# Moving the preparation of the second half of the tokens, one early product and the loads of the last product's h

## The chip, the cores and the metric

The kernel runs on one core of a Trainium2 chip. Its time is the device time of one execution in microseconds; several executions are made, and their median is given. A core has five engines that each work through their own list of instructions in order and wait for each other through semaphores: TensorE (PE in the profile), VectorE (DVE), ScalarE (ACT), GpSimd (POOL) and SyncE (SP), which issues nearly all of this kernel's transfers.

## The reference

For 2048 tokens (2 x 1024) of width 512, in float32:

```python
xn = layernorm(x)                              # no weights
s  = xn @ (weight * block_mask).T              # 512 x 512, mask in blocks of 32 x 32
nx = xn * rsqrt(mean(xn * xn) + 1e-5) * ln_w
h  = silu(nx @ gate_w.T) * (nx @ up_w.T)       # gate_w, up_w: 1792 x 512
g  = silu(h @ down_w.T)                        # down_w: 512 x 1792
out = x + s * g
```

The mask of a block is 1 where any of its elements is above zero. Of `setup_inputs`, what matters is the sizes above.

## The kernel before

**Products.** All matrix products are made with a scheme of seven products in place of eight (a Strassen form), applied twice: an outer level with products q = 1 to 7 and an inner level with products m = 1 to 7. A group g holds 128 rows of gate and 128 of up; there are G = 7 groups, and an eighth (g = G) that is the masked weight. For each group and each q, `instance(j, g, q, ...)` makes seven 128x128 by 128x512 products into PSUM banks called x, y and z (tags X, Y, Z; V is for everything else). j is the place in the order: first q = 1 and 2 for all eight groups (j = 0 to 15), then for each group q = 6, 5, 7, 3, 4. So "x_1" in the text is the bank x of instance j = 1. Within an instance the products have offsets 0, 2, 3, 4, 6, 8 and 12 (m = 1, 5, 2, 6, 3, 7, 4), so that two instances interlace and PE makes one product per position.

**Sums around a product.** After m = 1, `seed` copies x (into bank z for j > 0, so that z accumulates on it; into a slot named s1 for j = 0). `snap` takes a copy of an unfinished bank, plus the sums of the product before (`prior`); `total` adds such copies to the finished bank. With no prior these are ACT copies, else DVE sums. A product that goes on in a bank has to wait for the snapshot out of it.

**Tokens.** The 2048 tokens are four blocks t of 512, each four tiles of 128. A block is prepared by `load_x`, `stats` (DVE), `factors` (which has a square root on ACT), `normalise`, `transpose` (PE, into a bank pt_t_c for each 128 columns c), `evacuate` (ACT), and by sums of blocks, `outer_b` and `inner_b`. Blocks 0 and 1 are needed from the first product on, blocks 2 and 3 from j = 16 on.

**Order.** Nothing is scheduled by a tool. Each step is filed with a position by `at(pos, fn, ...)`, and at the end the steps are issued in the order of their positions; each engine executes its own in that order. One position is about 0.86 us; `T(us)` turns a planned time into a position, and `EARLY` holds positions for single products and seeds of the first instances that differ from the rule. `SILU = 26.2` is the earliest position of a silu.

**The h of the last product.** For each group, h and sums of it are written to `h_dram`. The last product, with `down_w`, loads them by sets (`load_h(q, slots, part)`); its first set, q = 1, comes in six parts: four of 768 KB (b11, b12, b22, b21) and two of 256 KB (e0, e1). SP's list holds these loads among stores of h, loads of each group's weights (`load_block`, L274, from in_gu), of the pieces of down_w (`outer_d`, L499), of the q = 1 and 2 sums (acc_dram, L462) and of h again (L465).

**Slots.** `mem` is one large SBUF tile, cut into slots of 128x512 by name (B1, q, v5 and so on); whoever takes a slot again waits for its readers.

Banks come from a pool with a number for each tag (`PSB`): X has three, Y two, Z one and V two, so a new tile with a tag waits for the readers of an old one.

Of the kernel before, what the change touches and what calls it, by code (L numbers as in the profile page):

```python
# [9 lines left out]
I32 = mybir.dt.int32  # L10
# [21 lines left out]
def tile_masked_linear_gated_ffn(  # L32
# [11 lines left out]
    nc = tc.nc  # L44
# [21 lines left out]
    EARLY = {}  # L66

    def at(pos, fn, *args):
        events.append((pos, len(events), fn, args))
# [5 lines left out]
    mem = big.tile([P, sum(n for _, n in RINGS), W], F32, tag="mem", name="mem")  # L75
# [5 lines left out]
    F = first_slot  # L81
# [11 lines left out]
    def bank(tag, name):  # L93
        return ps.tile([P, W], F32, tag=tag, name=name, bufs=PSB[tag])

    def add(eng, o, a, b, op=ALU.add):
        eng.tensor_tensor(o, a, b, op)  # L97

    dve, pool, act = nc.vector, nc.gpsimd, nc.scalar
# [68 lines left out]
    def rms_factor():  # L168

        def first():  # L170
            nc.vector.tensor_scalar_add(rms, agg[:, :, :, 1], EPS)
            nc.vector.reciprocal(rms, rms)
            nc.vector.tensor_mul(rms, agg[:, :, :, 1], rms)
            nc.vector.tensor_scalar_add(rms, rms, EPS)
        return [first, lambda: nc.scalar.activation(rms, rms, AF.Sqrt)]
# [115 lines left out]
    mrows = {}  # L291

    def load_mask(R, K):
        mrows[R, K] = mem[:, F["v5"] + 2 * R + K, :].bitcast(I32)
        nc.sync.dma_start(mrows[R, K], mask[R, K])

    mask_sums = small.tile([P, 4, 16], F32, tag="mask_sums", name="mask_sums", bufs=1)
# [35 lines left out]
    def instance(j, g, q, prior, dest, after):  # L333


        st = {}

        seeded = j > 0

        def mm(m, tag, key, first):  # L340
            if first and key not in st:
                st[key] = bank(tag, f"{key}_{j}")
            nc.tensor.matmul(st[key], weights(g, q, m), operand(q, m), start=first and not (key == "z" and seeded),  # L343
                             stop=True, skip_group_check=True)

        def seed():

            if seeded:
                st["z"] = bank("Z", f"z_{j}")
                nc.scalar.copy(st["z"], st["x"])  # L350
            else:
                st["s1"] = slot("s2", f"s1_{j}")
                nc.scalar.copy(st["s1"], st["x"])

        def snap(key, name, i):
            s = st[name] = slot(name, f"{name}_{j}")
            if prior is None:
                nc.scalar.copy(s, st[key])
            else:
                add(dve, s, st[key], prior(i))  # L360

        def total(key, name, i):
            if key == "z" and not seeded:
                name = "s1"
            if name:
                add(dve, dest(i), st[key], st[name])
            elif prior is None:
                nc.scalar.copy(dest(i), st[key])
            else:
                add(dve, dest(i), st[key], prior(i))  # L370

        at(EARLY.get((j, 0), 7 * j + 1), seed)
        for off, m, tag, first, snapshot, out in (
            (0, 1, "X", True, None, None),
            (2, 5, "Y", True, ("s5", 3), None),
            (3, 2, "Z", True, None, (None, 0)),
            (4, 6, "X", False, ("s2", 1), None),
            (6, 3, "Y", False, None, ("s2", 1)),
            (8, 7, "X", False, None, ("s5", 3)),
            (12, 4, "X", False, None, (None, 2)),  # L380
        ):
            key, pos = tag.lower(), 7 * j + off
            at(EARLY.get((j, m), pos), mm, m, tag, key, first)
            if snapshot:
                at(pos + 1, snap, key, *snapshot)
            elif out:

                pos += 2.3 if prior is None and m == 2 and seeded else 1
                at(pos, total, key, *out)
                after(out[1], pos)  # L390

# [278 lines left out]
    N = len(order)  # L670
    END = 7 * N
    T = lambda us: (us - 14.9) / 0.86
    EARLY.update({(0, 1): T(11.5), (0, 0): T(12.6), (1, 1): T(12.7), (0, 2): T(12.8)})
    SILU = 26.2
    at(T(-10), load_x, 0)
    at(T(-10), lambda: nc.sync.dma_start(lnw_sb, ln_w))
# [10 lines left out]
    def plan(pos, step, todo):  # L687
        for i, fn in enumerate(todo):
            at(pos + step * i, fn)
# [4 lines left out]
            nc.tensor.matmul(b[:, :P], ident, ident, start=True, stop=True, skip_group_check=True)  # L694

    at(T(1.4), lambda: warm(30, bank("V", "idle")))
    for t, p, step in ((0, T(8.2), 0), (1, T(13.4), 0), (2, 14.5, 1.3), (3, 22.0, 1.3)):
        plan(p, step, factors(t))
    for i in range(TT):
        half = act if i < 2 else dve  # L700
        at(T(4.5 + 0.85 * i), stats, 0, i)
        at(T(9.0 + 0.7 * (i % 2)), normalise, 0, i, half)
        at(T(10.1 + 0.8 * i), stats, 1, i)
        at(T(14.2 + 0.7 * (i % 2)), normalise, 1, i, half)
        for c in range(KC):
            at(T((10.2, 10.6, 11.0, 11.8)[c] + 0.1 * i), transpose, 0, c, (2, 3, 0, 1)[i], "XYYX"[c])
            at(T(15.3 + 0.4 * c + 0.1 * i), transpose, 1, c, (2, 3, 0, 1)[i], "XVVY"[c])
    at(T(6.0), scale_a, 0, 0, pool)
    at(T(8.2), scale_a, 0, 1, pool)
    for c in range(KC):  # L710
        at(T((10.7, 11.3, 11.9, 14.0)[c]), evacuate, 0, c, act)
        at((5.6, T(16.0), 6.0, 3.14)[c], evacuate, 1, c, act)
    for us, q, m in ((15.9, 1, 5), (16.6, 1, 6), (17.2, 1, 7), (17.8, 2, 5), (18.4, 1, 4), (19.0, 2, 6),
                     (19.6, 2, 7), (20.3, 2, 4)):
        at(T(us), inner_b, q, m, dve)
    for q in (1, 2):
        for k in (0, 1):
            for n in (0, 1):
# [1 line left out]
    at(T(16.4), scale_a, 1, 0)  # L720
    at(5.2, scale_a, 1, 1)
    for i in range(TT):
        at(9.6 + 1.2 * i, stats, 2, i)
        at(17.2 + 1.3 * i, stats, 3, i)
        at((30.2, 37.0, 40.9, 44.0)[i], normalise, 2, i, act)
        at(26.5 + 2.4 * i, normalise, 3, i, dve)
    plan(22.2, 1.3, rms_factor())

    for t, p0 in ((3, 37.5), (2, 51.5)):
        n = t % 2  # L730
        for k, c in enumerate((2, 3, 0, 1)):
            for i in range(TT):
                at(p0 + 2 * k + 0.01 * i, transpose, t, c, i, "V")
            if c >= 2:
                at(p0 + 2 * k + 1.2, evacuate, t, c, act)
            else:
                at(p0 + 2 * k + 1.2, outer_b, 5, c, n, dve)
                at(p0 + 2 * k + 1.21, outer_b, 7, c, n, dve)
    for k in (0, 1):
        for n in (0, 1):  # L740
            at(58, outer_b, 3, k, n, None)
    for n, p0 in ((1, 46), (0, 60)):
        for k in (0, 1):
            at(p0 + 1.5 * k, outer_b, 6, k, n, dve)
            at(p0 + 2.2 + 1.7 * k + (16 if n == 1 else 4), outer_b, 4, k, n, pool)
    for q, p in ((6, 63), (5, 70), (7, 78), (4, 90), (3, 113)):
        for off, m, eng in ((0, 5, dve), (3, 6, dve), (5.5, 7, pool), (7.5, 4, pool)):
            at(p + off, inner_b, q, m, eng)

# [29 lines left out]
        for off, fn in zip((8, 24.6, 26.05, 26.06, 26.07, 27.5, 30), outer_d(f)):  # L779
            at(7 * where[f, BLOCKS[0]] + off, fn)  # L780
    for i, (R, K) in enumerate(QUADS):
        at(62, load_mask, R, K)
        at(68 + 1.5 * i, mask_rows, R, K)
    at(79.5, mask_blocks)
    at(120, rms_store)
    for t in range(NTT):
# [17 lines left out]
    QD, later = (F["a1"] + 4, F["acc"], F["s"] + 5), {}  # L804
    for o, q in enumerate(DOWN):
        if o == 0:
            parts = [(p, 7 * where[4, 6] + 4 * k) for k, p in enumerate((b11, b12, b22, b21, e0, e1))]
        elif o == 1:
            parts = [(p, END - 22 + 7 * p[0]) for p in (b11, b21, e0, b12, b22, e1)]
        else:  # L810
            d = D(o - 2)
            parts = [(b11, d(4)), (b12, d(4) + 0.1), (b21, d(14)), (b22, d(21)), (e0, d(25) + 1), (e1, d(25) + 1.1)]
        for part, pos in parts:
            at(pos, load_h, q, (H0, H1)[o % 2], part)
        for k, m in enumerate((5, 6, 7, 4)):
            if o:
                at(D(o - 1)((3, 8, 12, 18)[k]) + 0.3, inner_h, q, m, TS[(4 * o + k + 3) % 5])
            elif m in (6, 4):
                at(END + {6: -1.95, 4: 7.5}[m], inner_h, q, m, first_t[m])
        if o == 0:  # L820
            for k in range(K3):
                in_bank, sums = first_h(q, k, first_t[5], first_t[7])
                at(END - 24.4 + 7 * k, in_bank)
                at(END - 22.95 + 7 * k, sums)
        at((END - 29.8, END - 14, END + 7)[o] if o < 3 else D(o - 2)(4), load_d, q, QD[o % 3])

        def weight_sums(q=q, i=F["q"] + 2 - 3 * (o % 2), o=o):
            for k, fn in enumerate(inner_d(q, i)):
                later[o, k] = fn
        for k in range(4):  # L830
            pos = END + (-6, -4.8, 2, 4)[k] if o == 0 else D(o - 1)(10) + 2.5 * k
            if k == 0:
                at(pos, weight_sums)
            at(pos, lambda o=o, k=k: later[o, k]())
# [81 lines left out]
```

## Time and profile before

| | us |
|---|---|
| median of 3 runs | 516.2 (515.59 to 516.71) |
| the profiled execution, its time | 516.81 |
| the profiled execution, its span | 515.0 |
| PE busy | 507.4 |
| DVE busy | 383.6 |
| POOL busy | 339.3 |
| ACT busy | 179.3 |

The span is from the first to the last instruction; the time has what lies around it too. TensorE's granted clock is at full speed in all of it. In the profile a product of 128x512 is two matmul instructions[...]. "L97" is a line of the kernel before; many sums have that one line, that of the helper `add`. In the time line, a row can hold several instructions of a kind that follow each other (x2 and so on).

### The profile page before, as it was taken

To read this page: it belongs to the slowest core of one execution; us is meant where nothing else is said; L and a number is where in the kernel's file an instruction comes from. 1 tells how busy PE (TensorE), PEld (TensorE's weight loads), DVE (VectorE), ACT (ScalarE), POOL (GpSimd) and SP (SyncE) were. 2 spreads that over 40 slices of the span, in tenths; PEclk is the share of its full clock that TensorE was granted. 3 is DMA by queue.
4 is the path that set the end of the run, shared out by engine and by line. 5 is a ranking of instruction groups with operands and counts; after the bars stand their busy time and mean duration, and the time that the engine had idled before them with its cause. 6 is when DMAs were issued, how large, how long until landed. Compare 5 with 4: busy or idle time off the path is not lost. (4 is left out here: it accounts for less than half of the span.)

```text
span 515.0 us, 4942 instructions
## 1 busy us (share of the span) xinstructions
PE 507.4 (99%) x1277; PEld 231.5 (45%) x1277; DVE 383.6 (74%) x587; ACT 179.3 (35%) x343; POOL 339.3 (66%) x280
## 2 busy tenths in 40 slices
PE   8999999999999999999999999999999999999997
PEld 8444544444444444444434444444444444444444
DVE  5898789766986969789596978978846655467726
ACT  3657554642536344353533524331100101001111
POOL 5422229952695978869598799977653654739960
PEclk9999999999999999999999999999999999999999
DMA  8335456459157584676987568399997699466472
GB/s 311 139 123 204 164 200 232 181 215 325 73 208 223 223 285 178 229 247 198 357 342 272 198 228 282 144 316 397 348 357 275 190 352 342 158 253 204 156 233 82
DMA packets 60460, 121.59 MB, mean 236 GB/s; under 512 B 5760, under 2 KB 13328, under 8 KB 58384
## 3 DMA queue, kind: packets, MB, share of 16 engines
q1 hardware_dynamic: 60144, 120.75, 66.1%
q10 hardware_dynamic: 288, 0.52, 0.3%
q8 instruction: 10, 0.16, 0.2%
q14 instruction: 18, 0.15, 0.1%
HBM read 75.11 MB, written 46.15 MB: 235 GB/s over the span
## 5 line engine op out<-in xcount | busy, mean ns | idle before, releaser
L97 POOL TENSOR_TENSOR mem<-mem 128x512 f32<-128x512 f32 (+4 forms) x243 | 303.6, 1271 | 139.0 <-ACT mem L264 45.6
L343 PE MATMUL x<-mem 128*128 128x512 f32 x448 | 214.3, 595 | 1.1 <-DVE mem L97 1.0
L343 PEld LDWEIGHTS x<-mem 128*128 128x128 f32 x448 | 83.4, 190 | 108.7 <-issue 85.2
L97 DVE TENSOR_TENSOR mem<-x,mem 128x512 f32<-128x512 f32 x136 | 92.1, 685 | 41.1 <-PE x L343 40.0
L343 PE MATMUL y<-mem 128*128 128x512 f32 x224 | 114.5, 592 | 0.1
L97 DVE TENSOR_TENSOR mem<-mem 128x512 f32<-128x512 f32 (+3 forms) x62 | 78.7, 1277 | 6.9 <-PE dx L586 3.6
L586 PE MATMUL dx<-mem 128*128 128x512 f32 x174 | 78.3, 592 | 0.0
L97 DVE TENSOR_TENSOR mem<-y,mem 128x512 f32<-128x512 f32 x96 | 65.8, 685 | 11.0 <-PE y L343 9.5
L343 PEld LDWEIGHTS y<-mem 128*128 128x128 f32 x224 | 42.2, 190 | 52.6 <-issue 47.4
L350 ACT COPY z<-x 128x512 f32<-128x512 f32 x55 | 31.5, 573 | 96.8 <-PE x L343 89.4
L343 PE MATMUL z<-mem 128*128 128x512 f32 x112 | 57.5, 594 | 0.7 <-ACT z L350 0.7
L586 PEld LDWEIGHTS dx<-mem 128*128 128x128 f32 x174 | 33.1, 190 | 41.6 <-issue 40.7
L586 PE MATMUL dy<-mem 128*128 128x512 f32 x98 | 44.5, 592 | 0.0
L404 ACT ACTIVATE gate<-mem 128x512 f32<-128x512 f32 x56 | 33.1, 601 | 28.2 <-DVE mem L97 23.8
L409 DVE TENSOR_TENSOR mem<-gate,mem 128x512 f32<-128x512 f32 x56 | 38.2, 683 | 4.4 <-POOL mem L97 4.2
L559 POOL TENSOR_TENSOR mem<-mem 128x512 f32<-128x512 f32 x16 | 24.7, 1545 | 16.7 <-DMA mem<-s_dram 16.6
L343 PEld LDWEIGHTS z<-mem 128*128 128x128 f32 x112 | 20.9, 190 | 26.8 <-issue 23.4
L569 ACT ACTIVATE silu<-mem 128x512 f32<-128x512 f32 x15 | 9.0, 602 | 64.6 <-DVE mem L97 48.3
L97 DVE TENSOR_TENSOR mem<-z,mem 128x512 f32<-128x512 f32 x41 | 28.0, 684 | 3.6 <-PE z L343 3.6
L586 PEld LDWEIGHTS dy<-mem 128*128 128x128 f32 x98 | 18.6, 190 | 23.4 <-issue 23.2
L97 DVE TENSOR_TENSOR mem<-dx,mem 128x512 f32<-128x512 f32 x16 | 11.1, 691 | 20.1 <-PE dx L586 20.1
L586 PE MATMUL dz<-mem 128*128 128x512 f32 x56 | 25.2, 592 | 0.0
(72 smaller groups left out, 286.7 us busy)
## 6 DMA issues: line engine op xcount, KB each, us to landing
h_dram<-mem SPq DMA_DIRECT2D x98, 256.0 KB, 2.1
mem<-h_dram SPq DMA_DIRECT2D x28, 768.0 KB, 6.7
mem<-in_gu SPq DMA_DIRECT2D x42, 256.0 KB, 4.7
acc_dram<-mem SPq DMA_DIRECT2D x8, 1024.0 KB, 4.3
mem<-acc_dram SPq DMA_DIRECT2D x8, 1024.0 KB, 4.8
s_dram<-mem SPq DMA_DIRECT2D x16, 256.0 KB, 5.0
mem<-s_dram SPq DMA_DIRECT2D x16, 256.0 KB, 6.6
mem<-in_x_t SPq DMA_DIRECT2D x16, 256.0 KB, 6.3
```

Source lines behind the costliest of these rows:

```text
L97: eng.tensor_tensor(o, a, b, op)
L343: nc.tensor.matmul(st[key], weights(g, q, m), operand(q, m), start=first and not (key == "z" and seeded), stop=True, skip_group_check=True)
L350: nc.scalar.copy(st["z"], st["x"])
L404: nc.scalar.activation(gate[key], t(), AF.Silu)
L409: nc.vector.tensor_mul(a(), gate[key], b())
L559: at_later.append(lambda: nc.gpsimd.tensor_tensor(s_tile, s_tile, rms_bc[t], ALU.mult))
L569: nc.scalar.activation(b[0][:, part], y[:, part] if source is None else source(), AF.Silu)
L586: nc.tensor.matmul(st[key], w(), b(), start=first and key != "z", stop=True, skip_group_check=True)
```

## The change

It does these things:

- All of the preparation of blocks 2 and 3 (stats, factors, normalise, transposes, sums) is filed later, most of it by 14 positions. Their square roots thereby come after the first silu. The mask's rows are loaded earlier, into slots of the name q, and reduced with more distance.
- z of instance 1 (`(1, 2)` in `EARLY`) is made in the first gap, after z of instance 0. It starts afresh in a Y bank, and is no longer seeded; x of instance 1 is instead added, with the prior, to a slot by a DVE sum (`seed`), and `total` of z is filed at position 7.0. The copy of pt_0_3 is filed earlier for it. pt_1_3 goes to a V bank, and its transposes come a little later. Two of the sums `inner_b` of q = 1 and 2 go from DVE to POOL.
- The six parts of h of the first set are loaded one per group behind the groups' weights: b11, b12, b22 and b21 with groups 1 to 4, e0 and e1 with group 5.

The diff, cut to its core (in unchanged order):

```diff
-        mrows[R, K] = mem[:, F["v5"] + 2 * R + K, :].bitcast(I32)
+        mrows[R, K] = mem[:, F["q"] + 2 * R + K, :].bitcast(I32)
...
-        seeded = j > 0
+        seeded = j > 1
...
-                st[key] = bank(tag, f"{key}_{j}")
+                st[key] = bank("Y" if key == "z" and j == 1 else tag, f"{key}_{j}")
...
-                nc.scalar.copy(st["s1"], st["x"])
+                if prior is None:
+                    nc.scalar.copy(st["s1"], st["x"])
+                else:
+                    add(dve, st["s1"], st["x"], prior(0))
...
+                if m == 2:
+                    pos = EARLY.get((j, "z"), pos)
...
-    EARLY.update({(0, 1): T(11.5), (0, 0): T(12.6), (1, 1): T(12.7), (0, 2): T(12.8)})
+    EARLY.update({(0, 1): T(11.5), (0, 0): T(12.6), (1, 1): T(12.7), (0, 2): T(12.8), (1, 2): T(12.9),
+                  (1, 0): 4.5, (1, "z"): 7.0})
...
-    for t, p, step in ((0, T(8.2), 0), (1, T(13.4), 0), (2, 14.5, 1.3), (3, 22.0, 1.3)):
+    for t, p, step in ((0, T(8.2), 0), (1, T(13.4), 0), (2, 36.0, 1.2), (3, 36.1, 1.2)):
...
-            at(T(15.3 + 0.4 * c + 0.1 * i), transpose, 1, c, (2, 3, 0, 1)[i], "XVVY"[c])
+            at(T((15.3, 15.7, 16.1, 16.9)[c] + 0.1 * i), transpose, 1, c, (2, 3, 0, 1)[i], "XVVV"[c])
...
-        at(T((10.7, 11.3, 11.9, 14.0)[c]), evacuate, 0, c, act)
+        at(T((10.7, 11.3, 11.9, 12.85)[c]), evacuate, 0, c, act)
...
-    for us, q, m in ((15.9, 1, 5), (16.6, 1, 6), (17.2, 1, 7), (17.8, 2, 5), (18.4, 1, 4), (19.0, 2, 6),
-                     (19.6, 2, 7), (20.3, 2, 4)):
-        at(T(us), inner_b, q, m, dve)
+    for us, q, m, eng in ((15.9, 1, 5, dve), (16.6, 1, 6, dve), (17.2, 1, 7, dve), (17.8, 2, 5, dve), (18.4, 1, 4, pool),
+                          (18.5, 2, 6, dve), (19.6, 2, 7, dve), (19.8, 2, 4, pool)):
+        at(T(us), inner_b, q, m, eng)
...
-        at(9.6 + 1.2 * i, stats, 2, i)
-        at(17.2 + 1.3 * i, stats, 3, i)
-        at((30.2, 37.0, 40.9, 44.0)[i], normalise, 2, i, act)
-        at(26.5 + 2.4 * i, normalise, 3, i, dve)
-    plan(22.2, 1.3, rms_factor())
-
-    for t, p0 in ((3, 37.5), (2, 51.5)):
+        at(14.0 + 2.5 * i, stats, 2, i)
+        at(25.0 + 3 * i, stats, 3, i)
+        at((44.0, 51.0, 55.2, 58.2)[i], normalise, 2, i, act)
+        at(40.5 + 2.4 * i, normalise, 3, i, dve)
+    plan(36.2, 1.2, rms_factor())
+
+    for t, p0 in ((3, 51.5), (2, 65.5)):
...
-    for n, p0 in ((1, 46), (0, 60)):
+    for n, p0 in ((1, 60), (0, 74)):
...
-    for q, p in ((6, 63), (5, 70), (7, 78), (4, 90), (3, 113)):
+    for q, p in ((6, 77), (5, 83), (4, 89), (7, 100), (3, 118)):
...
-        at(62, load_mask, R, K)
-        at(68 + 1.5 * i, mask_rows, R, K)
+        at(50, load_mask, R, K)
+        at(62 + 3.5 * i, mask_rows, R, K)
...
-            parts = [(p, 7 * where[4, 6] + 4 * k) for k, p in enumerate((b11, b12, b22, b21, e0, e1))]
+            parts = [(p, 7 * where[min(k, 4) + 1, 6] + 11) for k, p in enumerate((b11, b12, b22, b21, e0, e1))]
```

More of the change, by code (lines that the diff above doesn't have):

```diff
@@ L740, in tile_masked_linear_gated_ffn @@
         for n in (0, 1):
-            at(58, outer_b, 3, k, n, None)
-    for n, p0 in ((1, 46), (0, 60)):
+            at(72, outer_b, 3, k, n, None)
+    for n, p0 in ((1, 60), (0, 74)):
         for k in (0, 1):
```

## The prediction

> **What bounds the kernel now.** First the page's busy times and its chain: TensorE is busy for 507.4 of 515.0 us, and in the chain followed back from the end only PE has a large share.
>
> ```profile
> PE 507.4 (99%) x1277; PEld 231.5 (45%) x1277; DVE 383.6 (74%) x587; ACT 179.3 (35%) x343; POOL 339.3 (66%) x280
> ...
> PE 35%; DVE 2%; POOL 1%; issue 0%; ACT 0%; DVEq 0%; POOLq 0%
> ```
>
> The edits neither add nor drop a product: the same 128x512 products (two matmul passes, 0.86 us from one start to the next) and 64 transposes (0.11 us each). So only stretches in which PE has nothing to do can be won or lost. I read the time line for differences between PE starts above these two steps, then who ended each wait. They fall in three places.
>
> The first is the start, until the first half of the tokens runs steadily (time line; columns: start, duration, engine, line, operation, and in brackets the idle time before it with its releaser):
>
> ```profile
> 13.96 1.02 PE L343 MATMUL z<-mem 128*128 128x512 f32 x2
> ...
> 15.34 0.30 PE L155 MATMUL pt<-ident,mem 128*128 128x128 f32 x1 [0.36 <-DVE mem L146]
> ...
> 15.85 1.71 PE L155 MATMUL pt<-ident,mem 128*128 128x128 f32 x13 [0.20 <-DVE mem L146]
> ...
> 17.55 0.69 DVE L97 TENSOR_TENSOR mem<-pt,mem 128x512 f32<-128x512 f32 x1 [0.36 <-ACT mem L163]
> ...
> 20.19 1.11 PE L343 MATMUL x<-mem 128*128 128x512 f32 x2
> ...
> 21.39 1.10 PE L343 MATMUL y<-mem 128*128 128x512 f32 x2
> ...
> 22.35 0.68 DVE L97 TENSOR_TENSOR mem<-y,mem 128x512 f32<-128x512 f32 x1
> ...
> 22.99 1.13 PE L343 MATMUL z<-mem 128*128 128x512 f32 x2 [0.51 <-ACT z L350]
> ...
> 27.96 1.10 PE L343 MATMUL x<-mem 128*128 128x512 f32 x2 [0.41 <-DVE mem L97]
> ```
>
> The reader is to see holes: z of the first product ends its slot at 14.82 and the next work starts at 15.34 and, after one transpose, 15.85: 0.92 us. Then 0.34 before 21.39, 0.74 before 22.99, 0.11 after it, 0.57 before 27.96. From 17.55 VectorE runs without a break, one step each 0.60 us (17.55, 18.16, 18.76 and so on to 22.35): it paces this stretch.
>
> The second is small: at 82.6 to 88 us three PE steps are together 0.25 us too long, while DVE is busy 14.97 of the 15 us from 75 to 90. The third is near 257 us:
>
> ```profile
> 252.03 1.71 ACT L264 ACTIVATE mem<-mem,lnw_sb 128x256 f32<-128x256 f32 x4 [1.85 <-DMA mem<-in_gu]
> ...
> 257.48 1.13 PE L343 MATMUL z<-mem 128*128 128x512 f32 x2 [0.24 <-ACT z L350]
> ...
> 259.89 1.13 PE L343 MATMUL x<-mem 128*128 128x512 f32 x2 [0.43 <-DVE mem L97]
> ```
>
> Here 0.40, 0.10, 0.60 and 0.10 us of PE steps are lost, 1.2 in all (a product after a wait also has a first pass longer by 0.10). Four ordinary groups of 30.3 us lose 0.25 each, at 146, 176, 207 and 237, and don't have this. What is different is the queue on SP:
>
> ```profile
> 239.61 0.43 SPq L526 DMA_DIRECT2D mem<-h_dram  x1
> ...
> 243.43 0.70 SPq L526 DMA_DIRECT2D mem<-h_dram  x1
> ...
> 244.97 2.41 SPq L274 DMA_DIRECT2D mem<-in_gu  x4
> ```
>
> Two loads of 768 KB stand ahead of the group's weights. By the landing records the four blocks land at 252.01 to 254.01; one group before, at 217.41 to 221.49, which would be 247.7 to 251.8 here. ACT starts scaling at 252.03 instead of 250.1 (219.81 + 30.3), and the sums and the z seed behind it are late.
>
> **The Trainium skill.** "DMA: Bandwidth & Descriptors", section Queues, rings and completion order: descriptors of a ring are consumed in ring order. The trace agrees: behind the load of 243.43 everything lands in the order of issue, 256 KB each 0.65 us, the 768 KB themselves 2.0 to 2.7. "PSUM — Partial Sum Buffer", section PSUM bank collisions raise a hardware error: accesses of two engines to one bank must be kept apart, reads too. The trace shows such a wait at 17.55, where DVE waits 0.36 us for ACT's copy out of the bank it reads. "ScalarE: Activation LUTs", section What ACT_TABLE_LOAD costs: 1.28 us plus 1.38 of drain for each change of set. The trace has 1.28 us and no drain around it:
>
> ```profile
> 36.75 0.22 ACT L175 ACTIVATE rms<-rms 128x16 f32<-128x16 f32 x1 [1.28 <-DVE rms L174]
> 36.97 1.28 ACT L404 ACT_TABLE_LOAD   x1
> 38.27 1.12 ACT L404 ACTIVATE gate<-mem 128x512 f32<-128x512 f32 x2
> ```
>
> **The change, part by part.**
>
> *The start.* z of the second product now follows z of the first on PE. Its operand, the copy of pt_0_3, moves ahead of the square root on ACT: after the seed copy (12.87, next step 0.49 later) it runs 13.36 to 13.94, and its weights were scaled by POOL at 13.32. So it fills 14.82 to 15.68. The square root, ready at 13.88, loses at most 0.06; the first transpose moves from 15.34 to 15.68, but the second waits until 15.85 for the DVE normalise as before. Cost of the moved product: nothing. DVE's chain is unchanged at 16.50 and 17.55, since the transposes of pt_1_0 and pt_1_1 keep their times.
>
> Then: y_0 at 17.3; pt_1_3, now in a V bank, must wait for the reader of pt_1_1 (ends 18.24), so its four transposes run 18.30 to 18.74; x 18.74, y 19.60. The snapshot of x takes the slot of s1 and must wait for the sum of z_0 (ends 20.04): 20.10 to 20.69, so the next x starts at 20.76, against 20.19. y_1 takes y_0's bank, whose last reader is the eighth step of DVE's chain from 17.55: 17.55 + 7 x 0.60 + 0.69 = 22.44 (the two sums that moved to POOL make room for the new seed sum and the z_1 total). With the 0.15 that the trace shows from DVE's end to such a start, y_1 starts at 22.6, later than before by 1.2. But z_1 and its ACT seed are gone from behind it: x_1 23.5 (was 23.96), x_0 24.4, y_1 25.2, x_2 26.1 (26.53), x_1 27.0 (27.96), y_2 27.8 (28.89). The wait before 27.96 goes: with stats of the third block later, DVE takes x_1's snapshot at 24.6. POOL gets two sums of 1.27 us; it had 5.49 us idle before 21.00, and its group sums now end near 25.5 instead of 24.5, before y_2 needs the first. **Gain 1.08.**
>
> *Second half, 14 positions (12 us) later.* Stats, factors, normalise, transposes and sums keep their numbers and durations. The crowd on DVE thins: from position 70 to 84 ten extra steps of 0.6 beside some ten of the group (12.0 us of room), and the mask's reductions stand 3.5 positions apart. Followed step by step, every DVE result between 63 and 92 us is over 1 us ahead of the product that wants it: gain 0.25. POOL's crowd moves along: from position 77, 29.9 us of work; the second sum of the mask group, wanted at position 102, is ready near 97. On SP the four mask loads (1 MB, 2.7 us) pass ahead of stores and weights that have over 8 us. New: square roots now come after the first silu, so ACT has two more table loads. The first (near 45.7 to 47.0) stands between seeds of z. The second, near 51.7, has behind it a silu, a normalise (0.80) and the snapshot of y_6, done near 54.8; PE wants it at 55.2. **Cost 0, with 0.35 us of cover**; with the page's drain it would be late by 1.1. I take the trace's 1.28. Together **gain 0.25**, bounds -1.1 and +0.25.
>
> *h of the last product.* One load per group, issued behind the weights and behind the last store (in the group shown, after 221.0). Behind it stand the acc load (landed 229.63) and the 512 KB of h (231.15), moved by 2.0 to 2.7 us to at most 232.4 and 233.9. Their first users start at 239.48 (DVE, y snapshot) and 236.72 (POOL): covered. The weights no longer wait: **gain 1.2**. The next group's extra 0.16 (0.41 lost at 268.9 against 0.25) may go too; it is left to the range.
>
> Sum: 1.08 + 0.25 + 1.2 = 2.5. The profiled execution took 516.81 (span 515.0 and 1.8 around it), so 514.3; the median of the runs is 0.6 below it: **513.7**.
>
> **Rivals.** (a) The spread loads gain nothing: each delays its group a little, 0.3 us over four groups or the 1.2 returns. Against it the 2.8 us of cover at POOL; then 1.3, to 514.9. (b) The table loads end the wait: with the drain the y_6 snapshot is 1.1 late, 514.8. For it the page, against it the trace. (c) **Slower**: the spread loads meet a queue fuller than I assume, and POOL gets its h late in each of four groups. POOL idles 1.3 us later in that group, at 246.8, so from a landing past 236.72 + 1.3 = 238.0 (4.1 beyond mine) PE pays, taken at the 1.2 that the one disturbed group lost, in four groups: 4 x 1.2, less the 1.2 and the 1.3 won elsewhere, is 2.3 more, 518.5. Against it: before, the same bytes came within 16 us, now within 120. (d) It doesn't do what it says: the copy of pt_0_3 comes too late and z_1 pushes the transposes. It has 0.9 us of cover; at 0.9 late the gain at the start is about 0.2, 514.6.
>
> **Numbers.** 0.2% (1.0 us) is about what a measurement of this kernel can tell from no change. Likeliest case 0.70, 513.7; (a) 0.12, (b) 0.07, (d) 0.05, (c) 0.06. Shown runs scatter by 0.5 around their median; (a), (b) and (d) end near the edge of 515.2, so part of them counts as the same: faster 0.86, same 0.08, slower 0.06. The range takes in the left-out 0.16, the scatter below, and (a), (b), (d) above: 512.8 to 515.4.
>
> **What would show it.** Right: a z product at 14.8 and no PE hole until about 20.5; y_1 near 22.6 and no wait before x near 27; four ACT_TABLE_LOADs and no PE wait near 55; weights of the fifth group landing within 5.5 us of issue, no PE hole over 0.2 near 256 to 259. Wrong: PE waits for ACT at 52 to 60, POOL waits for h_dram loads, or new holes in groups that had only the 0.25.

## The result, and the profile after

The kernel after takes **514.45 us** (median of 6 runs, 514.33 to 514.50), the kernel before 516.46 (6 runs, 515.59 to 517.28): ratio 0.9961, 95% interval 0.9948 to 0.9973. A later comparison gave 514.55 (5 runs) against 516.59 (25 runs), ratio 0.9962, interval 0.9950 to 0.9975. So the gain of the medians is 2.0 us. The profiled execution took 514.33 with a span of 512.5; that of before 516.81 and 515.0, so those two differ by 2.5.

The page of the kernel after, busy times:

```profile
PE 506.2 (99%) x1277; PEld 231.2 (45%) x1277; DVE 380.8 (74%) x586; ACT 181.7 (35%) x344; POOL 340.5 (66%) x282
```

The number of PE instructions is what it was; what went is time between them. The waits of PE in the kernel after (engine, line, releaser; us in total, times, longest):

```profile
PE idle L700 <- POOL ident masks.py:199: 1.3, 1, 1.3
PE y L343 <- DVE mem L97: 0.7, 1, 0.7
```

Apart from the idle stretch at the very start, the wait of y for DVE is the only one over half a microsecond, and no wait for ACT is listed. The start, in the time line of the kernel after (start, duration, engine, line, operation, and the idle time before it with its releaser):

```profile
13.82 1.88 PE L343 MATMUL z<-mem 128*128 128x512 f32 x4
...
14.25 0.45 DVE L138 SCALAR_TENSOR_TENSOR nb<-agg,scl 128x4 f32<-128x4 f32 x1
...
14.74 1.01 DVE L146 TENSOR_SCALAR mem<-mem,scl,nb 128x512 f32<-128x512 f32 x2
...
15.54 1.97 PE L155 MATMUL pt<-ident,mem 128*128 128x128 f32 x12
...
17.73 0.69 DVE L97 TENSOR_TENSOR mem<-pt,mem 128x512 f32<-128x512 f32 x1 [0.36 <-ACT mem L163]
...
20.32 0.59 ACT L361 COPY mem<-x 128x512 f32<-128x512 f32 x1 [0.57 <-DVE mem L97]
...
20.96 1.13 PE L343 MATMUL x<-mem 128*128 128x512 f32 x2
...
22.75 1.10 PE L343 MATMUL y<-mem 128*128 128x512 f32 x2 [0.66 <-DVE mem L97]
...
27.98 1.02 PE L343 MATMUL y<-mem 128*128 128x512 f32 x2
```

z now stands four times in a row from 13.82 (two passes of each product), and PE goes on to the transposes at 15.54. Two gaps are new or moved: 0.27 us before 20.96, where the snapshot of x on ACT waited 0.57 for DVE, and 0.83 before 22.75. Each is followed by a first pass that is 0.075 to 0.105 us longer than the usual 0.43. Smaller losses, together 0.33, stand around y_0 from 17.24 to 18.65. The gap before x near 27 is gone, and y_2 starts at 27.98 instead of 28.89.

The third place, near 257 us, in the time line of the kernel after:

```profile
243.69 1.83 SPq L274 DMA_DIRECT2D mem<-in_gu  x4
...
248.96 1.70 ACT L264 ACTIVATE mem<-mem,lnw_sb 128x256 f32<-128x256 f32 x4
...
249.83 0.44 SPq L531 DMA_DIRECT2D mem<-h_dram  x1
...
255.95 1.02 PE L343 MATMUL z<-mem 128*128 128x512 f32 x2
...
256.27 19.73 POOL L97 TENSOR_TENSOR mem<-mem 128x640 f32<-128x640 f32 x15 [0.19 <-PE y L343]
...
256.81 1.88 PE L343 MATMUL x<-mem 128*128 128x512 f32 x4
...
259.38 1.88 PE L343 MATMUL x<-mem 128*128 128x512 f32 x4
```

The weights' four issues come first, the load of h six microseconds later. By the landing records the four blocks land at 246.36 to 249.18, and ACT begins scaling at 248.96 with no wait for a DMA before it, where in the kernel before it began at 252.03 after 1.85 us of waiting. PE has no gap from 250 to 265, and POOL works without a break.

### The profile page after: what moved, and what is told of

Same layout as the page of the kernel before. It is cut to its first block, busy times and chain, and to the rows that moved or that the text cites. A ratio compares the mean times of both kernels' runs of the same rounds, so it can differ in the third digit from the quotient of the medians.

```text
span 512.5 us, 4939 instructions
## 1 busy us (share of the span) xinstructions
PE 506.2 (99%) x1277; PEld 231.2 (45%) x1277; DVE 380.8 (74%) x586; ACT 181.7 (35%) x344; POOL 340.5 (66%) x282
## 5 line engine op out<-in xcount | busy, mean ns | idle before, releaser
L97 POOL TENSOR_TENSOR mem<-mem 128x512 f32<-128x512 f32 (+4 forms) x245 | 305.8, 1270 | 136.7 <-ACT mem L264 37.6
L97 DVE TENSOR_TENSOR mem<-x,mem 128x512 f32<-128x512 f32 x137 | 92.6, 684 | 42.2 <-PE x L343 41.1
L97 DVE TENSOR_TENSOR mem<-mem 128x512 f32<-128x512 f32 (+3 forms) x60 | 75.6, 1266 | 7.2 <-PE dx L591 4.4
L97 DVE TENSOR_TENSOR mem<-y,mem 128x512 f32<-128x512 f32 x96 | 65.7, 684 | 10.0 <-PE y L343 8.7
L97 DVE TENSOR_TENSOR mem<-z,mem 128x512 f32<-128x512 f32 x41 | 28.0, 682 | 3.4 <-PE z L343 3.4
L97 DVE TENSOR_TENSOR mem<-dx,mem 128x512 f32<-128x512 f32 x16 | 11.0, 690 | 20.1 <-PE dx L591 20.1
```

## The experiments

Times are medians. The kernel before was run beside each group: 516.85 (45 runs) for the first four, 516.52 (34) for the next four, 516.59 (25) for the last three. "Gap" means time between two starts on PE above the usual step.

**The moment to count from.** Of each kernel one execution was profiled, and these don't start alike: VectorE begins to normalise the second block (L146, at 14.74 in the time line above) between 14.56 and 15.02 us, and what follows shifts with it. From that moment on, the two kernels that were profiled twice repeat within 0.03 us. Of the others there is one trace each, and later waits can still differ between executions, as one case below shows. The table counts from there, in us, to the start of y_2 and to the end of the span:

| kernel | to y_2 | to the end |
|---|---|---|
| before | 14.33 | 500.47 |
| before, with the start alone | 13.66 | 499.75 |
| before, with the second half alone | 13.69 | 499.40 |
| before, with the loads of h alone | 14.33 | 499.08 |
| before, with the loads bunched behind the weights | 14.33 | 499.71 |
| after, twice | 13.24, 13.24 | 497.81, 497.83 |
| after, with the loads ahead of the weights | 13.24 | 498.41 |
| after, with the loads bunched behind the weights | 13.24 | 497.81 |
| after, with two copies more on ScalarE | 13.24 | 498.80 |
| after, with y_1 in a V bank, twice | 12.34, 12.34 | 496.91, 496.93 |
| the same, with the total of z_0 earlier | 12.32 | 496.91 |

**The three parts, each alone.** First the start alone, put into the kernel before:

```diff
-        seeded = j > 0
+        seeded = j > 1
...
+                  (1, 0): 4.5, (1, "z"): 7.0})
```

and with it the Y bank, the sum on DVE, the V bank of pt_1_3, the earlier copy of pt_0_3 and the two sums on POOL, as in the diff above.

> The kernel before with the start alone changed: z of instance 1 in the first gap, its Y bank, the DVE seed sum, pt_1_3 in a V bank, two inner sums on POOL. Theory (the gains are separate PE holes that add up): z at 13.8 to 14.0 in four passes without a hole, y_1 near 22.7, and the hole near 257 (1.2 us) stays; the hole before x near 27 stays shut only if stats of the third block, still early here, leave DVE free in time: if not, up to 0.5 us of the start's 0.9 is given back. Span 514.1 to 514.6. Rival (z_1 in the gap is paid back whole by the wait of y_1, and the gain at the start comes from stats moved later): span 515.0, y_2 as late as before, at 28.9.

Measured: 516.27 (515.42 to 517.47), ratio 0.9989, interval 0.9982 to 0.9996, span 514.6. The time line of PE in this kernel:

```profile
27.52 1.12 PE L343 MATMUL x<-mem 128*128 128x512 f32 x2 [0.15 <-DVE mem L97]
...
257.04 1.12 PE L343 MATMUL z<-mem 128*128 128x512 f32 x2 [0.23 <-ACT z L350]
...
259.45 1.12 PE L343 MATMUL x<-mem 128*128 128x512 f32 x2 [0.43 <-DVE mem L97]
```

The gap before x near 27 stays in part (0.32 and a first pass 0.10 longer), because the stats of the third block still stand in DVE's way. By the table y_2 comes 0.67 earlier, so the rival, in which the wait of y_1 pays all of it back, is out. The gaps near 257 stay as well.

The second half alone, later by 14 positions:

```diff
-    for t, p, step in (..., (2, 14.5, 1.3), (3, 22.0, 1.3)):
+    for t, p, step in (..., (2, 36.0, 1.2), (3, 36.1, 1.2)):
...
-        at(9.6 + 1.2 * i, stats, 2, i)
+        at(14.0 + 2.5 * i, stats, 2, i)
```

and the other positions of blocks 2 and 3 and of the mask.

> The kernel before with the second half's preparation alone moved 14 positions. Theory: z_1 stays in line with its hole (0.74) before it; with the stats out of the way the wait before x near 27.96 goes or shrinks (0.57 and 0.07 of pass), the 0.25 at 83 to 88 goes, the hole near 257 stays. Span 514.1 to 514.5. Rival (the shift only moves DVE's crowd): new PE holes of 0.2 or more between 90 and 110 us, span 515.0 or more.

Measured: 515.97 (515.20 to 516.91), ratio 0.9985, interval 0.9978 to 0.9992, span 514.1. PE's time line:

```profile
23.16 1.12 PE L343 MATMUL z<-mem 128*128 128x512 f32 x2 [0.51 <-ACT z L350]
...
26.69 1.88 PE L343 MATMUL x<-mem 128*128 128x512 f32 x4
28.41 1.02 PE L343 MATMUL y<-mem 128*128 128x512 f32 x2
...
256.62 1.13 PE L343 MATMUL z<-mem 128*128 128x512 f32 x2
```

The wait of z for its seed stays. The gap before x near 27 (0.57, and 0.07 of first pass) is gone, and y_2 comes 0.64 earlier. PE has no gap over 0.06 between 84 and 145 us, so DVE's crowd did no harm in its new place, against the rival.

Alone, the two parts gain 0.67 and 0.64 ahead of y_2; together, in the kernel after, they gain 1.09. The 0.22 in between is counted twice: the start alone already shortens the gap near 27 from 0.64 to 0.42, and the second half alone closes all of it. So well over a third of the gain that I had filed under the start needs the other edit.

The loads of h alone:

```diff
-            parts = [(p, 7 * where[4, 6] + 4 * k) for k, p in enumerate((b11, b12, b22, b21, e0, e1))]
+            parts = [(p, 7 * where[min(k, 4) + 1, 6] + 11) for k, p in enumerate((b11, b12, b22, b21, e0, e1))]
```

> The kernel before with the six h loads alone spread over five groups behind the weights. Theory: the 1.2 us at 257 to 260 go and the next group's extra 0.16 too, the start and 83 to 88 stay as before: span 513.6 to 513.9, time about 1.3 under before. Rival (the loads cost each of four groups a little): holes of more than 0.25 at about 176, 207, 237 and 267 us, span 514.3 or more.

Measured: 515.71 (515.38 to 515.80), ratio 0.9974, interval 0.9965 to 0.9984, span 513.8. PE's time line:

```profile
28.14 1.10 PE L343 MATMUL x<-mem 128*128 128x512 f32 x2 [0.40 <-DVE mem L97]
...
258.12 1.88 PE L343 MATMUL x<-mem 128*128 128x512 f32 x4
```

The start is as before, the gaps near 257 to 260 are gone, the next group loses its ordinary 0.25, and no group loses more than 0.26, against the rival. Counted to the end, the three parts gain 0.72, 1.07 and 1.39, together 3.18, where the kernel after gains 2.66: they overlap. The start has 0.22 of this, and 0.17 lies near 257, where the second half alone has a gap of 0.23 before z in place of 0.40; the rest I didn't follow. Something else came with the loads: 10 runs lie within 0.42 us, where 45 of the kernel before spread over 2.3.

**Place or spreading?** The edit to the loads does two things: it spreads them over five groups, and it puts each behind its group's weights. Two kernels take one of them away from the kernel after. Spread, but ahead of the weights:

```diff
-7 * where[min(k, 4) + 1, 6] + 11
+7 * where[min(k, 4) + 1, 6] + 4
```

> The kernel after with one change: each of the first five 768 KB loads of h is issued just ahead of its group's expert weights on the same queue instead of just behind them. Theory (what matters is that the 768 KB stand behind the weights, the urgent load): the weights of four or five groups land some 2.0 to 2.7 us later; the slack between landing and first use in a group was about 2.4 us in the profile before, so each of those groups starts its first product 0 to 0.5 us late, and the time goes up by 0 to 2 us, likeliest 0.5 (about 515). Rival (only the bunching of the loads into one group cost time, not their place): no group shows an extra wait, 514.4.

Measured: 515.14 (514.43 to 515.51), ratio 0.9974, interval 0.9966 to 0.9982. One group's time line on ACT and PE:

```profile
220.12 1.71 ACT L264 ACTIVATE mem<-mem,lnw_sb 128x256 f32<-128x256 f32 x4 [1.05 <-DMA mem<-in_gu]
...
226.83 2.27 PE L343 MATMUL x<-mem 128*128 128x512 f32 x4
```

In this group the first block of weights, issued at 213.70, lands at 220.09, 6.4 us later; in the kernel after it takes 3.1 (213.40 to 216.53). ACT waits 1.05 for it, and PE has 0.29 and 0.10 of gap inside the four x passes (2.27 instead of 1.88) and 0.15 more in the next gap. In the fifth group the first block is late as well, 5.1 us after its issue instead of 2.7, and PE doesn't notice. So the place costs 0.55 in one group of this execution, just over the 0 to 0.5 per group expected, and nothing in the others; the median is 0.6 above the kernel after, as is the time to the end in the table.

Behind the weights, but all six in the fifth group again:

```diff
-7 * where[min(k, 4) + 1, 6] + 11
+7 * where[4, 6] + 11 + 0.01 * k
```

> The kernel after with one change: all six 768 KB loads of h stand in one group, the fifth, as before, but behind that group's expert weights. It separates bunching from order. Theory (bunching: some 11 us of transfers ahead of the 1 MB acc and the 512 KB h of the next group): acc lands near 267 and h near 268 to 269, POOL, which wants that h near 264 to 265, waits 3 us or so and passes up to 2 us of it to TensorE; time 514.5 to 516.5, and its runs scatter by over 1 us as those of the kernel before do. Rival (order alone decides: the weights come first, so no product is late): no gap on TensorE near 257 to 270, time 514.4 and scatter under 0.5.

Measured: **514.30** (4 runs, 514.21 to 514.66), ratio 0.9964, interval 0.9950 to 0.9977: as good as spread, and equal to it in the table. (Of the six loads, four are of 768 KB and two of 256 KB; this expectation and the next call all six 768 KB.) My theory of the bunching was wrong, though its transfers came nearly as late as I had said: acc lands at 266.55 and h at 267.85. The time line of SP's queue, POOL and PE:

```profile
249.52 5.71 SPq L531 DMA_DIRECT2D mem<-h_dram  x6
...
256.20 9.64 POOL L97 TENSOR_TENSOR mem<-mem 128x640 f32<-128x640 f32 x7 [0.20 <-PE y L343]
267.99 7.65 POOL L97 TENSOR_TENSOR mem<-mem 128x512 f32<-128x512 f32 x6 [2.14 <-DMA mem<-h_dram]
...
256.74 1.88 PE L343 MATMUL x<-mem 128*128 128x512 f32 x4
...
265.32 2.12 PE L343 MATMUL x<-mem 128*128 128x512 f32 x4
```

POOL waits 2.14 us for the load, and PE has only the 0.25 of an ordinary group at 266. POOL had that much slack, with little to spare: its lag delays the weights of the next group too, in a way shown below, and their first block lands at 278.75, 0.42 before ACT begins to scale it at 279.17.

The same question put to the kernel before, with only the place changed:

```diff
-7 * where[4, 6] + 4 * k
+7 * where[4, 6] + 11 + 0.01 * k
```

> The kernel before with one change: its six 768 KB loads of h stay in one group, the fifth, but all stand behind that group's expert weights instead of the first two ahead of them. Theory (the place behind the weights is what counts, not the spreading): the 1.2 us of gaps near 257 to 260 go and the next group's extra 0.16, as with the spread loads alone (515.7), so 515.6 to 515.8, and the runs scatter by about 0.4 instead of 2. Rival (in the kernel before, whose ScalarE has normalising to do around the same time, the spreading counts too): 516.2 to 516.9, scatter over 1.

Measured: 515.62 (21 runs, 515.37 to 516.49), ratio 0.9983, interval 0.9977 to 0.9990: the median of the spread loads, 515.71, without any spreading. The scatter came out at 1.1, not at 0.4. The profiled execution, 516.26, is one from the tail, and the time line shows what that looks like:

```profile
270.15 10.12 POOL L97 TENSOR_TENSOR mem<-mem 128x512 f32<-128x512 f32 x8 [2.88 <-DVE mem L97]
...
278.25 1.82 SPq L274 DMA_DIRECT2D mem<-in_gu  x4
...
280.98 0.91 ACT L264 ACTIVATE mem<-mem,lnw_sb 128x256 f32<-128x256 f32 x2 [0.28 <-DMA mem<-in_gu]
...
288.45 2.28 PE L343 MATMUL x<-mem 128*128 128x512 f32 x4
```

No gap near 257 to 260. But POOL starts at 270.15 after 2.88 of idle (put down to DVE, but its h landed at 270.02), and a group later PE has gaps that the kernel with the spread loads lacks: 0.40 near 289.6, and 0.18 more than usual at 298.6. The first can be followed. On SP the stores of POOL's sums stand ahead of the next group's weights. They begin at 271.45, where in the kernel with the spread loads they begin at 268.48, and the weights are issued at 278.25 instead of 275.28. The first block lands at 280.96 instead of 278.47, so ACT waits for it, and the DVE sum that x near 289.6 waits for starts at 288.87 instead of 288.25. Bunched loads can thus cost PE time a group later, by way of POOL and SP's list.

**ScalarE's cover near 55 us.** Two copies more, ahead of the snapshot of y_6 and behind the second table load:

```diff
+    for _ in range(2):
+        at(44.0, lambda: nc.scalar.copy(mem[:, F["q"] + 4, :], xt[2, 1]))
```

> The kernel after with two 128x512 copies more on ScalarE (each some 0.6 us, to a tile that a copy fills already with the same values), right ahead of the snapshot of y_6 and behind the second table load. Theory (ScalarE's lead over TensorE there is 0.34 us): the snapshot of y_6 comes about 1.2 us later, TensorE waits 1.2 - 0.34 = 0.85 us ahead of y_6's next pass near 55.4, some of it perhaps made good by idle time later on; time 515.0 to 515.4. Rival (ScalarE's lead is larger than the profile shows, since other work of TensorE moves up): under 0.2 us, 514.5.

Measured: 515.31 (20 runs, 514.72 to 515.93), ratio 0.9977, interval 0.9970 to 0.9983. First the time line of the kernel after, then that of this one:

```profile
51.94 1.28 ACT L409 ACT_TABLE_LOAD   x1
53.23 0.60 ACT L409 ACTIVATE gate<-mem 128x512 f32<-128x512 f32 x1
...
54.47 0.57 ACT L361 COPY mem<-y 128x512 f32<-128x512 f32 x1
...
55.44 1.02 PE L343 MATMUL y<-mem 128*128 128x512 f32 x2
```

```profile
54.59 1.25 ACT L735 COPY mem<-mem 128x512 f32<-128x512 f32 x2
55.75 0.58 ACT L361 COPY mem<-y 128x512 f32<-128x512 f32 x1
...
56.48 1.10 PE L343 MATMUL y<-mem 128*128 128x512 f32 x2 [0.75 <-ACT mem L361]
```

The snapshot starts 1.28 later, of which 0.12 is this execution's later start, and PE has 0.91 of gap, plus a slow first pass of 0.075. So ScalarE's lead there was 1.28 - 0.12 - 0.91 = 0.25. The kernel after shows the same in another way: its snapshot ends at 55.04 and PE starts at 55.44, and of these 0.40 PE takes 0.15 from the end of a snapshot that it waits for (here 56.33 to 56.48). The table load at 51.94 takes 1.28 us, and the next activation follows within 0.02.

**The wait that is left.** y_1 takes the bank of y_0, so at 22.75 PE waits for DVE. In this kernel it takes a V bank:

```diff
-                st[key] = bank("Y" if key == "z" and j == 1 else tag, f"{key}_{j}")
+                st[key] = bank({("z", 1): "Y", ("y", 1): "V"}.get((key, j), tag), f"{key}_{j}")
...
-(1, "z"): 7.0
+(1, "z"): 10.5
```

> The changed kernel with y of instance 1 in a V bank and the total of z_1 filed at 10.5 in place of 7.0. Theory (the new 0.8 us hole before y_1 is only the wait for y_0's bank and its place in DVE's chain): y_1 then waits for the reader of pt_1_3, done near 20.8, and starts right behind x at 21.9 to 22.0; span 511.5 to 511.9, 0.8 to 1.0 under the changed kernel. Rival (DVE's chain is the bound, and the hole returns at the next product that needs a DVE step): y_1 early, but holes of together 0.6 or more before x_0, y_1 or x_1 between 23 and 28 us; span 512.3 to 512.6.

Measured: **513.59** (4 runs, 513.08 to 513.67), ratio 0.9934, interval 0.9920 to 0.9949. In its time line y_1 starts right behind x:

```profile
21.05 4.26 POOL L97 TENSOR_TENSOR mem<-mem 128x512 f32<-128x512 f32 x5 [1.10 <-DVE mem L97]
...
21.13 1.12 PE L343 MATMUL x<-mem 128*128 128x512 f32 x2
...
22.09 1.02 PE L343 MATMUL y<-mem 128*128 128x512 f32 x2
```

This and the kernel after were then run side by side on one chip:

> The kernel after, unchanged, beside more runs of the kernel before. The spans of the two profiled executions differ by 2.5 us, the medians of the first comparison by 2.0. If that is only because the kernel before scatters, the gain of the medians over many runs is 2.0 to 2.5 (ratio 0.9952 to 0.9961) and the kernel after stays within 0.4 of 514.4.

> The kernel with y_1 in a V bank and the total of z_1 at 10.5, on the same chip as the kernel after. Theory (the 0.83 us gap and the first pass before y near 22.8 are all that it saves): 0.7 to 0.9 below the kernel after. Rival (other waits give part of it back, or the difference of the first two comparisons was one of chips): under 0.5.

Measured: the kernel after 514.55 (514.48 to 514.69), the one with y_1 in a V bank 513.53 (512.94 to 513.59). That is 1.0 less, in the spans as well (512.8 and 511.8). Counted from normalising it is 0.90, just the gap (0.825) and the first pass (0.075). Beside 25 runs of the kernel before the gain of the kernel after is 2.04, so the 2.0 of the first comparison was no accident.

One gap of the start is left in this version, 0.27 before x at 21.13. The total of z_0 is moved one step ahead to free the slot:

```diff
-                  (1, 0): 4.5, (1, "z"): 10.5})
+                  (1, 0): 4.5, (1, "z"): 10.5, (0, "z"): T(17.7)})
```

> The kernel with y_1 in a V bank (e4_y1_in_v), and the total of z_0 moved one VectorE step earlier, so that the snapshot of x, which waits for a slot, is made 0.6 us sooner. Theory (the 0.27 us gap and the 0.10 us first pass ahead of x near 21.1 wait for that slot): the gap goes, span 511.4 to 511.5 (e4: 511.8), time 513.2 to 513.3. Rival (the step that z_0's total is moved past becomes late, and TensorE waits for that instead): 513.5 to 513.9.

Measured: 513.23 (5 runs, 513.04 to 513.72), ratio 0.9944, interval 0.9932 to 0.9957: not to be told from the version without this edit. The time line says why:

```profile
19.81 1.48 DVE L97 TENSOR_TENSOR mem<-pt,mem 128x512 f32<-128x512 f32 x2
...
21.37 4.26 POOL L97 TENSOR_TENSOR mem<-mem 128x512 f32<-128x512 f32 x5 [1.31 <-DVE mem L97]
...
22.81 2.11 PE L343 MATMUL x<-mem 128*128 128x512 f32 x4
...
23.80 0.30 PEld L343 LDWEIGHTS x<-mem 128*128 128x128 f32 x2 [0.79 <-POOL mem L97]
```

The gap before x is gone, but the DVE steps that were moved past now end at 21.29 instead of 20.98, and POOL's sums start at 21.37 instead of 21.05; 0.11 of both is this execution's later normalising. The weights of x at 23.80 wait for POOL: 0.16 of new gap and 0.075 of first pass, against the 0.27 won. In the table the two versions end alike, so the rival held.

## Why the prediction was right, and where its steps were off

**The sum.** Forecast 1.08 + 0.25 + 1.2 = 2.5; between the two profiled executions, 2.48. That they agree so closely is in part luck. Counted from normalising, the gaps give 1.09 + 0.19 + 1.2 + 0.16 = 2.64 (2.66 in the table). The 0.16 had been left to the range, and 0.18 was lost before that moment, for a reason that is met without the change too.

**The start, 1.08 forecast, 1.09 measured.** z of the second product did cost nothing, and with no wait. Against the clock of the profile this term looks like 0.91 (y_2 at 27.98 instead of 28.89), and the step "DVE's chain is unchanged at 16.50 and 17.55" looks wrong: the chain stood at 16.68 and 17.73. But in both kernels these are 1.94 and 2.99 after normalising began, so that step held. It was normalising that began later, at 14.74 instead of 14.56, and one small DVE step ahead of it makes the difference. First the kernel before, then the one after:

```profile
14.36 0.16 DVE L138 SCALAR_TENSOR_TENSOR nb<-agg,scl 128x4 f32<-128x4 f32 x1
...
14.56 1.23 DVE L146 TENSOR_SCALAR mem<-mem,scl,nb 128x512 f32<-128x512 f32 x2
```

```profile
12.75 1.93 POOL L97 TENSOR_TENSOR mem<-mem 128x128 f32<-128x128 f32 x4
...
14.25 0.45 DVE L138 SCALAR_TENSOR_TENSOR nb<-agg,scl 128x4 f32<-128x4 f32 x1
```

This happens without the change too: in the three other kernels whose start is that of the kernel before, the same step took 0.26, 0.27 and 0.46, and normalising began at 14.72 to 14.77. The traces show what it goes with. In the ten in which the step took over 0.2 us, a POOL sum (L97) was under way when it began, and the step ended 0.02 us after that sum. In the three in which it took 0.16, no such sum was under way, or it ended within 0.02. So its length depends on how the lists of DVE and POOL happen to meet in an execution. Apart from these 0.18 everything is within 0.04 of where the prediction put it: the snapshot of x at 20.32 (20.10 forecast), x at 20.96 (20.76), y_1 at 22.75 (22.6), y_2 at 27.98 (27.8). The kernel with y_1 in a V bank showed the wait for y_0's bank by taking it away.

One cost of the moved copy was put too low for some executions. The square root behind it on ACT was to lose at most 0.06. In the profiled execution of the kernel after it lost 0.03, but with the two copies more it lost 0.53 and with the total of z_0 earlier 0.39, since there the copy stood ahead of it when it was ready.

Also off was the place of part of this term. The prediction counted the gap before x near 27 to the start and gave the reason, the stats of the third block; by the single parts, the 0.42 of it that the start leaves is won by the second half.

**The second half, 0.25 forecast, 0.19 measured.** One of the three long steps, a first pass of z, keeps its extra 0.056. The crowd on DVE and POOL did move. The stretch from 75 to 90 us in the windows of the two kernels, first after, then before (columns: window, its length, then PE, PEld, DVE, ACT and POOL busy, with instruction counts, PE's clock, DMA share and GB/s):

```profile
75.00:90.00 15.00, 15.00 (x46) 7.33 (x45) 13.64 (x23) 7.28 (x14) 5.12 (x6) 1.00 0.52 193
```

```profile
75.00:90.00 15.00, 15.00 (x38) 6.57 (x37) 14.97 (x23) 5.87 (x12) 15.00 (x13) 1.00 0.64 233
```

**The table loads, cost 0 with 0.35 of cover.** The cost was 0; the cover was 0.25, by the two copies, as the 0.15 between a snapshot's end and PE's start had been counted at 0.05. The Trainium skill's page "ScalarE: Activation LUTs", section What ACT_TABLE_LOAD costs, names a drain beside the load; after both loads here the next activation starts 0.01 us later, and no run of this case shows one. Had it come, PE would have paid, as in rival (b). This is an estimate from the copies: with the snapshot 1.16 us later by them PE lost 0.91, and 0.075 of first pass.

**The loads of h, 1.2 forecast.** Right in size, and the next group's 0.16, left to the range, went too. What carried it was "the weights no longer wait", the place in the queue; the spreading adds nothing to the median that these runs can tell. Acc and h landed at 231.25 and 232.59, inside the bounds of 232.4 and 233.9 given; as PE is 1.1 us ahead there, this is 2.6 to 2.8 later for it, the upper end of the 2.0 to 2.7 forecast. Rival (c) was mispriced: it let PE pay as soon as POOL was 1.3 us late. With all six loads bunched behind the weights POOL idled 2.14 us, and PE lost nothing. But its path exists: in the kernel before, with the loads bunched, 2.88 us of POOL's idling came with gaps of PE a group later.

**From the sum to the median.** The profiled execution ought to take 514.3 and took 514.33. I then took off 0.6, the distance of the profiled execution of before to its median over three runs. That was the step with the largest error. Over 45, 34 and 25 runs the median of before is 516.85, 516.52 and 516.59, so its profiled execution was nearly typical, and three runs that spread by 1.1 us could not tell. Without that step the forecast would have been within 0.25 of both medians of the kernel after.

**What stays open.** The gains of the parts by their ratios are 0.11%, 0.15% and 0.26%, together 0.52%, and the whole is 0.38 to 0.39%. The intervals are wide enough for both, but the traces say the same: 3.18 us for the parts, 2.66 for the whole. The medians gain 2.0, less than the 2.66; of the kernel before only one execution has a trace, so what its faster executions do otherwise isn't known. Why it scatters is only partly settled: with the loads spread behind the weights alone, 10 runs lie within 0.42 us, and of the kernel after 11 runs within 0.36; but the two copies on ScalarE bring 1.2 us back without touching a load. Why a DVE step ends with a POOL sum isn't shown by any run here.

## What to carry to other kernels

Put a prefetch that nobody wants soon behind the urgent loads of its queue before thinking of spreading it: here the place alone was worth as much in the median as place and spreading together, though bunched loads left a tail. To compare two traces, look for an event behind which executions of one kernel repeat, and count from it: from the start of the span the start's gain read 0.91, and what the two parts gained there alone, 0.41 and 0.48, seemed to add up to it; from normalising on it was 1.09, and the parts, 0.67 and 0.64, overlap. Don't shift a sum by an offset to a median of three scattered runs. When a late engine releases the last wait, look at what it does next: of two rearrangements of the start tried here, one gained 0.9 to 1.0 us and the other next to nothing, since it delayed the step that POOL was waiting for.

## What was unexpected of the hardware

A tiny DVE operation on 128x4 elements took 0.16 us in some executions and up to 0.46 in others, with the same operands: when a POOL sum of 128x128 had more than 0.02 us to go as it began, it ended 0.02 us after that sum, in ten traces of ten. The first pass of a product after a wait is longer by 0.075 to 0.105 us in all these kernels, so a gap costs about a tenth of a microsecond more than its length. And a kernel of 516 us whose profiled gaps come to a few microseconds can scatter by 2.3 us from run to run, while moving six loads in a queue brings it to 0.4 (over 45 and 10 runs).
